# Layer 1's sums by node, as products of 32 columns in four quarters of the TensorE array

## The chip, the cores and the metric

The kernel runs on one core of one Trainium2 chip. The metric is the device time of one launch in microseconds; several runs are taken and their median is the kernel's time. All arrays are float32 unless said otherwise.

## The reference, cut to what matters

The reference is a stack of eight layers over 3125 nodes and 50,000 edges: four graph layers with a feed-forward (mixture) layer behind each. The edges arrive sorted by their receiving node. Two of the graph layers meet in the part of the kernel that is changed:

```python
def _L0_gnn_ref(h, weight, norm, src, dst, rel_type):
    transformed = jnp.einsum('ni,rio->rno', h, weight)      # 16 relations
    msg = transformed[rel_type, src] * norm
    return jax.ops.segment_sum(msg, dst, num_segments=h.shape[0])
...
def _L1_gnn_ref(node_z, node_feats, senders, receivers, edge_weight, edge_feats, ...):
    cut = 0.5 * (jnp.cos(edge_weight * jnp.pi / CUTOFF) + 1.0)
    cut = cut * (edge_weight < CUTOFF).astype(jnp.float32)
    W = (edge_feats @ W_dist + b_dist) * cut[:, None]
    x_j = embed_table[node_z][senders]
    msgs = x_j * W
    agg = jax.ops.segment_sum(msgs, receivers, num_segments=node_feats.shape[0])
    return jnp.concatenate([node_feats, agg], axis=1) @ W_comb + b_comb
```

`agg`, the sum of layer 1's messages by receiving node, is what the change is about. It needs nothing of layer 0's result, so the kernel computes it in the same pass over the edges as layer 0's sums.

## The kernel before, in words

**Stage one** (`stage_one`, L788) makes layer 0's graph sum, layer 0's mixture, layer 1's graph layer and the tables for layer 2, all in one loop. Nodes are cut into 25 tiles of 126 (the last holds 101), and a tile into 21 windows of six nodes (the last tile has 17), 521 windows in all. A window is the up to 128 edges that end in its six nodes; they lie one to a partition. A word table `tab` in DRAM holds for each node its normalised features and its embedding, 512 words.

For each window `k` the loop takes these steps:

- `fetch_rows` (L825): POOL starts an indirect DMA (the helper's line, L136) that gathers the 128 senders' rows of `tab` into a tile `g`. `G_BUFS` (L89) of these tiles go round, so the gathers run that many windows ahead, each as soon as the tile it takes is free.
- `fetch_feats` (L833): SP starts a DMA of the window's edge features into `f`, six windows ahead.
- `build` (L842): VectorE (DVE) builds two selection matrices, two windows ahead: `s0` (128 edges by 96 columns, six nodes by sixteen relations, weighted by `norm`; L850) and `s1` (128 edges by the 126 nodes of the tile, weighted by the cutoff; L852).
- `window` (L858): TensorE (PE) multiplies the two halves of the gathered features by `s0` into `c` (L866). ScalarE (ACT) copies `c` into `aT`, for two windows at a time (L870). PE multiplies the edge features by `W_dist` into `pw` (L873), and DVE multiplies `pw` by the gathered embeddings, in place in the second half of `g` (L875).
- `add_up` (L879), two windows behind: PE multiplies `s1` by that half of `g` and adds it up in a PSUM bank `agg` over the tile's windows (L884). After the last one ACT copies `agg` out to `ag` (L890).

After a tile's windows come eight `weigh` steps (L892): 32 products of `aT` with the sixteen relations' weights `w_rel` (L897). Windows and `weigh` steps together are 29 slots for a tile. In each slot `between` (L1117) takes a few steps of `route`, `experts` and `combine`, which carry the pairs of tiles already summed through layer 0's mixture and layer 1's second half, and steps of `background`, which finds where later tiles' edges begin and prepares the later layers.

The order in which each engine gets its work in this stage is the order in which this loop writes it (`tc.manual_schedule`); nothing is moved by a scheduler. PSUM has two buffers for `c`, two for `pw`, one for `agg`, one for the weighed sum `f` and two (`w`) for all the rest. After stage one the other layers follow, each after the last has been drained; the change does not touch them.

The part of the loop that fixes the order around the change, for a window step `j` of tile `t`:

```python
                build()
                window(k)
                if j >= 2:
                    add_up(k - 2)
                k += 1
```

The functions that the change touches, whole:

Of the kernel before, what the change touches and what calls it, by code (L numbers as in the profile page):

```python
# [9 lines left out]
F32 = mybir.dt.float32  # L10
# [3 lines left out]
OP = mybir.AluOpType  # L14
# [5 lines left out]
P = 128  # L20
N = 3125
NT = 25
NP = NT * P
NV = N - (NT - 1) * P
D = 256
# [20 lines left out]
TN = 126  # L46
TV = N - (NT - 1) * TN
NX = NT * TN
GN = 6
GC = TN // GN  # L50
GW = GN * 16
GL = -(-TV // GN)
# [3 lines left out]
F_SRC, F_CODE, F_NORM, F_DST, F_CUT, F_W0, F_W1, F_EID = range(8)  # L56
# [29 lines left out]
Q_SRC, Q_DST, Q_TYP, Q_W, Q_W1, Q_EW, Q_EID = range(7)  # L86
RW = 8

G_BUFS, F_BUFS = 10, 6  # L89
PERIOD = 2 * (GC + 8)  # L90
META_AT = 10
BG_EVERY = 3
# [3 lines left out]
def tile_gnn_ffn(ctx: ExitStack, tc: tile.TileContext, a: dict, out: bass.AP):  # L96
    nc = tc.nc
# [14 lines left out]
    def ps(tag, shape):  # L112
        return banks["pool"].tile(shape, F32, name=tag, tag=tag, bufs=banks["bufs"][tag])
# [21 lines left out]
    def gather(dst, table, idx):  # L135
        return nc.gpsimd.indirect_dma_start(  # L136
            out=dst, out_offset=None, in_=table, in_offset=bass.IndirectOffsetOnAxis(ap=idx, axis=0))
# [14 lines left out]
    iota_f = per.tile([P, P], F32, name="iota_f")  # L152
# [248 lines left out]
    for i in range(5):  # L401
        xg = pp.tile([P, 5, D], F32, name=f"n_x{i}")
        t = 5 * i
        m = 5 if i < 4 else 4
# [22 lines left out]
    for t in range(0, NT, 4):  # L427
        n = min(4, NT - t)
# [36 lines left out]
    with tc.If(uns > 0):  # L465

        rec = dram.tile([E, RW], F32, name="rec")
        with tc.tile_pool(name="srt", bufs=1) as ep, tc.tile_pool(name="srt2", bufs=2) as eb, \
# [25 lines left out]
            for b in range(ET // BT):  # L494
                s = slice(b * BT, (b + 1) * BT)
                n = BT * EP
# [9 lines left out]
                for i in range(BT):  # L506
                    j = b * BT + i
# [15 lines left out]
                at = eb.tile([EP, BT, 64], F32, name="s_attr")  # L523
# [137 lines left out]
    cur = start_norm(0)  # L661
# [3 lines left out]
    for i in range(5):  # L665
# [12 lines left out]
        cur = nxt  # L678
# [109 lines left out]
    def stage_one(late, cp, eb):  # L788
# [4 lines left out]
        def bank():  # L793
            return ps("w", [P, 2, D])
# [8 lines left out]
        def meta(t):  # L803
            pt = bank()[:, 0, :R1]
            nc.tensor.transpose(pt, raw.pop(t), ident[:R1, :R1])
            mt = eb.tile([P, 5, GC], F32, name="m_mt")
            si = eb.tile([P, GC], I32, name="m_si")
            un = eb.tile([P, GC], F32, name="m_un")
            nc.vector.tensor_copy(mt, pt.rearrange("p (f j) -> p f j", f=5))
            nc.vector.tensor_copy(si, mt[:, F_SRC])  # L810
            c, d, u = mt[:, F_CODE], mt[:, F_DST], mt[:, F_CUT]
            nc.vector.tensor_scalar_add(d, d, -float(TN * t))
            stt(c, c, -16.0 * TN * t, j96, op0=OP.add, op1=OP.subtract)

            nc.vector.tensor_tensor(un, d, j6, op=OP.is_lt)
            nc.vector.tensor_mul(u, u, un)
            mts[t], sis[t] = mt, si


        wins = [(t, j) for t in range(NT) for j in range(GL if t == NT - 1 else GC)]  # L820
        rows, feats, sums = {}, {}, {}
        agg_of = {}
        nxt = {"g": 0, "f": 0, "s": 0}
# [1 line left out]
        def fetch_rows():  # L825
            k = nxt["g"]
            if k < len(wins):
                nxt["g"] += 1
                t, j = wins[k]
                rows[k] = eb.tile([P, 2 * D], F32, name="g", bufs=G_BUFS)  # L830
                gather(rows[k], tab, sis[t][:, j : j + 1])

        def fetch_feats():  # L833
            k = nxt["f"]
            if k < len(wins):
                nxt["f"] += 1
                t, j = wins[k]
                feats[k] = eb.tile([65, P], F32, name="f", bufs=F_BUFS)
                v = nc.values_load(mixI[j : j + 1, t : t + 1], engines={EN.SP}, min_val=0, max_val=E)
                nc.sync.dma_start(feats[k], a["attr_t"][:, bass.ds(v, P)])  # L840

        def build():  # L842
            k = nxt["s"]
            if k < len(wins):
                nxt["s"] += 1
                t, j = wins[k]
                m = mts[t]
                s0 = eb.tile([P, GW], F32, name="s0", bufs=4)
                s1 = eb.tile([P, TN], F32, name="s1", bufs=5)
                nc.vector.tensor_scalar(s0, iota_f[:, :GW], m[:, F_CODE, j : j + 1], m[:, F_NORM, j : j + 1],  # L850
                                        op0=OP.is_equal, op1=OP.mult)
                nc.vector.tensor_scalar(s1, iota_f[:, :TN], m[:, F_DST, j : j + 1], m[:, F_CUT, j : j + 1],  # L852
                                        op0=OP.is_equal, op1=OP.mult)
                sums[k] = s0, s1

        cur = {}

        def window(k):  # L858
            t, j = wins[k]
            last = k + 1 == len(wins) or wins[k + 1][0] != t  # L860
            if j % 2 == 0:
                cur["c"] = ps("c0", [P, 2, D])
            pc, g = cur["c"], rows[k]
            o = (j % 2) * GW
            for h in range(2):
                nc.tensor.matmul(pc[:, h, o : o + GW], g[:, h * P : (h + 1) * P], sums[k][0], start=True, stop=True)  # L866
            if j % 2 or last:
                n = o // GW + 1
                b = (j - n + 1) * GN
                nc.scalar.copy(aT[:, :, :, b : b + n * GN].rearrange("p k r n -> p k n r"),  # L870
                               pc[:, :, : n * GW].rearrange("p k (n r) -> p k n r", r=16))
            pw = ps("pw", [P, D])
            nc.tensor.matmul(pw, feats.pop(k), wd, start=True, stop=True)  # L873
            fetch_feats()
            nc.vector.tensor_tensor(g[:, D:], pw, g[:, D:], op=OP.mult)  # L875

        ag_of = {}

        def add_up(k):  # L879
            t, j = wins[k]  # L880
            last = k + 1 == len(wins) or wins[k + 1][0] != t
            if j == 0:
                cur["agg"] = ps("agg", [P, D])
            nc.tensor.matmul(cur["agg"][:TN], sums.pop(k)[1], rows.pop(k)[:, D:], start=(j == 0), stop=last)  # L884
            fetch_rows()
            if last:
                q, i = t // 2, t % 2
                if i == 0:
                    ag_of[q] = eb.tile([P, 2, D], F32, name="ag", bufs=3)
                nc.scalar.copy(ag_of[q][:TN, i, :], cur["agg"][:TN])  # L890

        def weigh(t, i):  # L892
            if i == 0:
# [15 lines left out]
        def load_x(q):  # L909
            n = size(q)  # L910
            x = x_of[q] = eb.tile([P, 2, D], F32, name="x", bufs=3)
            if n == 1:
                nc.gpsimd.memset(x[:, 0, :], 0.0)
                nc.sync.dma_start(x[:TV, 0, :], a["x"][2 * q * TN :, :])
            else:
                nc.sync.dma_start(x[:TN], a["x"][2 * q * TN : 2 * (q + 1) * TN, :].rearrange("(t p) d -> p t d", p=TN))

        def load_e(q, i):
            n = size(q)
            e = e_of[q, i] = eb.tile([P, 2, D], F32, name=f"e{i}", bufs=1)  # L920
            nc.sync.dma_start(e[:TN, :n], rows126(ex, 2 * q, n)[:, :, i * D : (i + 1) * D])
# [214 lines left out]
        k = 0  # L1136
        for t in range(NT):
            n = GL if t == NT - 1 else GC
            for j in range(n):
                build()  # L1140
                window(k)
                if j >= 2:
                    add_up(k - 2)
                k += 1
                if j == 3 and t + 1 < NT:
                    raw[t + 1] = meta_load(t + 1, wb)
                if j == META_AT and t + 1 < NT:
                    meta(t + 1)
                if j == 14 and t % 2 == 0:
                    load_x(t // 2)  # L1150
                if j == 18 and t == 1:
                    beyond(eb, bank())
                if t % 2 and j == 19:
                    load_e(t // 2, 0)
                between()
            for i in range(8):
                weigh(t, i)
                if i < 2:
                    add_up(k - 2 + i)
                if i == 7 and (t % 2 or t == NT - 1):  # L1160
                    if t == NT - 1:
                        load_e(t // 2, 0)
                    flows.append(Flow(t // 2))
                between()
# [262 lines left out]
    with tc.tile_pool(name="f1", bufs=1) as fp, tc.tile_pool(name="f1b", bufs=2) as fb, psums(mm=3, y=3, tp=2):  # L1427
# [30 lines left out]
        for sh in range(28, -1, -4):  # L1458
            n = 8 if sh == 28 else 16
# [82 lines left out]
        for t in range(NT):  # L1542
            nc.tensor.matmul(pl.rearrange("p i k -> p (i k)"), fl[:, t, :], vals[:, t].rearrange("p i k -> p (i k)"),
                             start=(t == 0), stop=(t == NT - 1))
# [554 lines left out]
    with tc.tile_pool(name="g2", bufs=2) as gp, \  # L2099
# [60 lines left out]
        xin, rows = {t: At() for t in order2}, {t: [] for t in order2}  # L2160
# [118 lines left out]
        with tc.manual_schedule(engines={EN.PE, EN.DVE, EN.Activation, EN.Pool, EN.SP}):  # L2279
# [4 lines left out]
            last = pl.add(4, experts2())  # L2284
# [13 lines left out]
    with tc.tile_pool(name="w3", bufs=1) as wp:  # L2298
# [9 lines left out]
        with tc.tile_pool(name="g3", bufs=2) as gp, psums(tp=3, mm=4):  # L2308
# [24 lines left out]
            rows = {}  # L2333
            with tc.manual_schedule(engines={EN.PE, EN.DVE, EN.Activation, EN.Pool, EN.SP}):
                for r in range(ROWS):
                    look(r)
                for t in range(NT):
# [149 lines left out]
```

## Time and profile before

| | us |
|---|---|
| median of 3 runs | 3864.81 |
| lowest and highest run | 3861.73, 3865.3 |
| the profiled execution's own time | 3860.75 |
| its span, from the first to the last instruction | 3859.0 |
| first product of stage one (`c`), and the end of the last tile's `weigh` steps | 97.7, 1761 |
| PE busy in the span | 2721.7 (71%) |
| PE busy on `agg` in the span | 334.1 |
| DVE, ACT, POOL busy in the span | 1987.3 (51%), 846.0 (22%), 1724.6 (45%) |

Each row of the profile's list of groups names line, engine, operation, the tiles written and read, the shape and the count; then the busy time in us and the mean duration of one in ns; then how long the engine stood idle just before them, and what ended most of that. A product of float32 tiles shows as two instructions (passes), each with its own weight load ("PEld"). Since products are pipelined, the duration of one is not its price: the distance between the starts of two that follow each other is. TensorE's granted clock is given as a share of full speed.

### The profile page before, as it was taken

How to read it: one execution, taken by the hardware profiler on the slowest of the kernel's cores; microseconds unless marked ns; L12 is line 12 of the kernel's file. 1: busy time of each engine (PE TensorE's matmuls, PEld its weight loads, DVE VectorE, ACT ScalarE, POOL GpSimd, SP SyncE). 2: the span in 40 equal slices, each digit the busy share in tenths (PEclk: the TensorE clock that was granted, in tenths of full speed). 3: DMA queues.
4: the chain of work that ended last, by engine and by line, in shares of the span. 5: the costliest groups of instructions: out<-in, count | busy, mean ns of one | idle time of the engine just before them, and what ended most of it. 6: DMA issues, size and time to landing. Idle time of an engine off the chain costs nothing. (4 is left out here: it accounts for less than half of the span.)

```text
span 3859.0 us, 46777 instructions
## 1 busy us (share of the span) xinstructions
PE 2721.7 (71%) x13015; PEld 2250.7 (58%) x13015; DVE 1987.3 (51%) x7555; ACT 846.0 (22%) x1771; POOL 1724.6 (45%) x1971
## 2 busy tenths in 40 slices
PE   3788999999899999999384227748483112237994
PEld 2666788887788888887373115537361111225673
DVE  4446665776566555544423755656664333337411
ACT  2111232322122322323121002213231000014331
POOL 0342233352144333330024777777435777762343
PEclk9778999998899999999687557869695555557997
DMA  5756544553243444431122437768452333333563
GB/s 181 235 157 208 165 136 128 153 159 84 67 120 94 137 115 122 116 109 47 49 87 73 110 104 241 212 185 261 161 172 76 105 105 105 105 93 116 172 212 97
DMA packets 274479, 518.31 MB, mean 134 GB/s; under 512 B 53068, under 2 KB 176106, under 8 KB 274194
## 3 DMA queue, kind: packets, MB, share of 16 engines
q0 software_dynamic: 103744, 303.34, 26.9%
q1 hardware_dynamic: 159598, 201.27, 16.9%
q10 hardware_dynamic: 10852, 10.45, 0.8%
q8 instruction: 113, 1.85, 0.2%
q14 instruction: 172, 1.41, 0.1%
HBM read 428.07 MB, written 86.78 MB: 133 GB/s over the span
## 5 line engine op out<-in xcount | busy, mean ns | idle before, releaser
L136 POOL DMA_INDIRECT g<-tab,m_si x521 | 499.1, 958 | 1013.7 <-PE agg L884 262.4
L136 POOL DMA_INDIRECT g_rows<-tab,srcI x413 | 401.7, 973 | 130.6 <-issue 101.8
L136 POOL DMA_INDIRECT g_row<-tab,srcI x413 | 391.0, 947 | 132.2 <-issue 118.1
L866 PEld LDWEIGHTS c<-s,g 128*128 128x128 f32 x2084 | 332.5, 207 | 95.6 <-issue 38.7
L897 PE MATMUL f<-w_rel,aT 128*126 128x256 f32 x1600 | 377.2, 385 | 0.0
L866 PE MATMUL c<-s,g 128*128 128x96 f32 x2084 | 334.2, 286 | 51.2 <-DMA g<-tab,m_si 21.6
L870 ACT COPY aT<-c 128x384 f32<-128x384 f32 (+1 forms) x273 | 230.0, 842 | 607.0 <-PE c L866 573.4
L873 PE MATMUL pw<-w_d,f 65*128 65x256 f32 x1042 | 354.1, 424 | 0.0
L2342 DVE TENSOR_TENSOR ACC<-ACC,g_row 128x256 f32<-128x256 f32 x413 | 175.7, 425 | 341.5 <-DMA g_row<-tab,srcI 340.9
L884 PE MATMUL agg<-g,s 128*126 128x256 f32 x1042 | 334.1, 403 | 5.4 <-DVE g L875 5.4
L897 PEld LDWEIGHTS f<-w_rel,aT 128*126 128x126 f32 x1600 | 302.3, 191 | 48.3 <-issue 4.0
L1617 PE MATMUL tp<-ident,ACC 128*128 128x128 f32 x50 | 16.6, 435 | 422.3 <-DVE ACC L2342 422.3
L1947 PE MATMUL mm<-ro_xt,ro_w 128*128 128x192 f32 (+3 forms) x1152 | 265.0, 378 | 46.8 <-ACT ro_h L2012 25.0
L875 DVE TENSOR_TENSOR g<-pw,g 128x256 f32<-128x256 f32 x521 | 218.9, 420 | 120.0 <-PE pw L873 117.5
L1951 PE MATMUL y<-ro_w,ro_h 128*96 128x256 f32 (+2 forms) x1152 | 267.3, 384 | 0.0
L1617 PEld LDWEIGHTS tp<-ident,ACC 128*128 128x128 f32 x50 | 7.2, 204 | 429.8 <-issue 354.1
L1947 PEld LDWEIGHTS mm<-ro_xt,ro_w 128*128 128x128 f32 x1152 | 200.6, 205 | 95.0 <-ACT ro_h L2012 33.0
L884 PEld LDWEIGHTS agg<-g,s 128*126 128x126 f32 x1042 | 211.4, 203 | 40.2 <-DVE g L875 5.8
L1951 PEld LDWEIGHTS y<-ro_w,ro_h 128*96 128x96 f32 (+2 forms) x1152 | 200.2, 179 | 43.5 <-issue 1.0
L1015 PE MATMUL w<-w,b_h 128*126 128x256 f32 x800 | 211.7, 389 | 3.5 <-ACT xt L928 1.7
L1006 PE MATMUL w<-xt,w 128*128 128x252 f32 (+1 forms) x832 | 206.8, 372 | 3.0 <-ACT b_h L1008 1.3
L2222 DVE SCALAR_TENSOR_TENSOR ACC<-g_rows,g_e,ACC 128x256 f32<-128x256 f32 x413 | 201.5, 488 | 13.6
(582 smaller groups left out, 4674.2 us busy)
## 6 DMA issues: line engine op xcount, KB each, us to landing
ro_w<-in_L_ffn_blocks SPq DMA_DIRECT2D x72, 514.0 KB
ro_w<-in_L_ffn_blocks SPq DMA_DIRECT2D x72, 512.0 KB
f<-in_attr_t SPq DMA_DIRECT2D x521, 32.5 KB
xg<-zero SPq DMA_DIRECT2D x78, 200.0 KB
b_at<-in_edge_attr SPq DMA_DIRECT2D x100, 125.0 KB
tabr<-v SPq DMA_DIRECT2D x12, 758.0 KB
g<-tab,m_si POOLq DMA_INDIRECT x521
g_rows<-tab,srcI POOLq DMA_INDIRECT x413
```

What stands on the lines that cost most here:

```text
L136: return nc.gpsimd.indirect_dma_start(out=dst, out_offset=None, in_=table, in_offset=bass.IndirectOffsetOnAxis(ap=idx, axis=0))
L866: nc.tensor.matmul(pc[:, h, o : o + GW], g[:, h * P : (h + 1) * P], sums[k][0], start=True, stop=True)
L870: nc.scalar.copy(aT[:, :, :, b : b + n * GN].rearrange("p k r n -> p k n r"), pc[:, :, : n * GW].rearrange("p k (n r) -> p k n r", r=16))
L873: nc.tensor.matmul(pw, feats.pop(k), wd, start=True, stop=True)
L875: nc.vector.tensor_tensor(g[:, D:], pw, g[:, D:], op=OP.mult)
L884: nc.tensor.matmul(cur["agg"][:TN], sums.pop(k)[1], rows.pop(k)[:, D:], start=(j == 0), stop=last)
L897: nc.tensor.matmul(cur["f"][:TN], aT[:, h, r, :], wrel[:, h, r, :], start=(r == 0 and h == 0), stop=(r == 15 and h == 1))
L1006: nc.tensor.matmul(ph, w["01"][:, e, k, i * P : (i + 1) * P], xt[:, k, : n * TN], start=(k == 0), stop=(k == 1))
L1015: nc.tensor.matmul(py, last[:, k, i * TN : (i + 1) * TN], w["02"][:, e - 1, k, :], start=(k == 0), stop=(k == 1))
L1947: nc.tensor.matmul(ph, w[:, o : o + P], xt[:, k, :], start=(k == 0), stop=(k == 1))
L1951: nc.tensor.matmul(py, h[:, i, s], w[:, i * D : (i + 1) * D], start=(i == 0), stop=(i == self.fc - 1))
L2222: stt(u, g[:, r, :D], e[:, r0 + r : r0 + r + 1], u, op0=OP.mult, op1=OP.add)
```

## The change

The sums by node are made in three batches for a tile, and with narrower selection matrices.

- A window's six nodes lie, for all but two of the windows, within one block of 32 of the tile's nodes. `quarter(j)` names it: `6 j // 32`, and none for windows 5 and 10, which straddle two blocks. For the others `s1` has only the 32 columns of that block, and its product goes to those 32 partitions of `agg`. Windows 5 and 10 keep a selection matrix over all columns, now 128.
- The windows of a tile are taken in another order: 1, 2, 6, 7, 11, 12, 16, 17, then 3, 4, 8, 9, 13, 14, 18, 19, then 0, 15, 20, 5, 10. Within a batch the sums are issued so that neighbours lie in different quarters (1, 6, 11, 16, and so on).
- `add_up` runs once for a batch instead of once for a window: eight products behind the tenth window, eight behind the eighteenth, five behind the second `weigh` step.
- DVE writes the multiplied embeddings into a new tile `mt` (11 buffers) instead of into `g`, so a `g` tile is free after that multiplication, and the next gather is issued in `window`. `G_BUFS` goes from 10 to 9. The 32-column `s1` has 13 buffers, the wide one 3.
- `c` is still copied out two windows at a time where two neighbours follow each other; the last five windows of a tile are copied one at a time. ACT gets 48 instructions more by that (two for each of the 24 full tiles).

```diff
-G_BUFS, F_BUFS = 10, 6
+G_BUFS, F_BUFS = 9, 6
...
-        wins = [(t, j) for t in range(NT) for j in range(GL if t == NT - 1 else GC)]
+        batches = ((1, 2, 6, 7, 11, 12, 16, 17), (3, 4, 8, 9, 13, 14, 18, 19), (0, 15, 20, 5, 10))
+        together = (((1, 6, 11, 16), (2, 7, 12, 17)), ((3, 8, 13, 18), (4, 9, 14, 19)), ((0, 15, 20), (5,), (10,)))
+
+        def quarter(j):
+            return None if j in (5, 10) else GN * j // 32
+
+        wins, second = [], []
+        for t in range(NT):
+            for b in batches:
+                for j in b:
+                    if t < NT - 1 or j < GL:
+                        second.append(bool(wins) and wins[-1] == (t, j - 1) and not second[-1])
+                        wins.append((t, j))
...
-                s1 = eb.tile([P, TN], F32, name="s1", bufs=5)
+                a = quarter(j)
+                a, m1 = (0, P) if a is None else (32 * a, 32)
+                s1 = eb.tile([P, m1], F32, name=f"s1_{m1}", bufs=13 if m1 == 32 else 3)
...
-            nc.vector.tensor_tensor(g[:, D:], pw, g[:, D:], op=OP.mult)
+            mt = mults[t, j] = eb.tile([P, D], F32, name="mt", bufs=11), sums.pop(k)[1]
+            nc.vector.tensor_tensor(mt[0], pw, rows.pop(k)[:, D:], op=OP.mult)
+            fetch_rows()
...
-            nc.tensor.matmul(cur["agg"][:TN], sums.pop(k)[1], rows.pop(k)[:, D:], start=(j == 0), stop=last)
-            fetch_rows()
+            agg, begun = cur["agg"], b > 0
+            for js in together[b]:
+                js = [j for j in js if (t, j) in mults]
+                for j in js:
+                    a = quarter(j)
+                    mt, s1 = mults.pop((t, j))
+                    o = agg if a is None else agg[32 * a : 32 * a + 32]
+                    nc.tensor.matmul(o, s1, mt, start=not begun, stop=(j == 10), skip_group_check=True)
+                begun = True
...
                 window(k)
+                k += 1
                 if j >= 2:
-                    add_up(k - 2)
-                k += 1
+                    at = wins[k - 2][1]
+                    if at in (3, 0):
+                        add_up(t, 0 if at == 3 else 1)
...
-                if i < 2:
-                    add_up(k - 2 + i)
+                if i == 1:
+                    add_up(t, 2)
```

More of the change, by code (lines that the diff above doesn't have):

```diff
@@ L848, in build @@
                 s0 = eb.tile([P, GW], F32, name="s0", bufs=4)
-                s1 = eb.tile([P, TN], F32, name="s1", bufs=5)
+                a = quarter(j)
+                a, m1 = (0, P) if a is None else (32 * a, 32)
+                s1 = eb.tile([P, m1], F32, name=f"s1_{m1}", bufs=13 if m1 == 32 else 3)
                 nc.vector.tensor_scalar(s0, iota_f[:, :GW], m[:, F_CODE, j : j + 1], m[:, F_NORM, j : j + 1],
                                         op0=OP.is_equal, op1=OP.mult)
-                nc.vector.tensor_scalar(s1, iota_f[:, :TN], m[:, F_DST, j : j + 1], m[:, F_CUT, j : j + 1],
+                nc.vector.tensor_scalar(s1, iota_f[:, a : a + m1], m[:, F_DST, j : j + 1], m[:, F_CUT, j : j + 1],
                                         op0=OP.is_equal, op1=OP.mult)
@@ L859, in window @@
             t, j = wins[k]
-            last = k + 1 == len(wins) or wins[k + 1][0] != t
-            if j % 2 == 0:
+            if not second[k]:
                 cur["c"] = ps("c0", [P, 2, D])
             pc, g = cur["c"], rows[k]
-            o = (j % 2) * GW
+            o = GW if second[k] else 0
             for h in range(2):
                 nc.tensor.matmul(pc[:, h, o : o + GW], g[:, h * P : (h + 1) * P], sums[k][0], start=True, stop=True)
-            if j % 2 or last:
-                n = o // GW + 1
+            if second[k] or k + 1 == len(wins) or not second[k + 1]:
+                n = 2 if second[k] else 1
                 b = (j - n + 1) * GN
@@ L874, in window, with add_up @@
             fetch_feats()
-            nc.vector.tensor_tensor(g[:, D:], pw, g[:, D:], op=OP.mult)
[L877 to L882, printed above, removed]
-                cur["agg"] = ps("agg", [P, D])
-            nc.tensor.matmul(cur["agg"][:TN], sums.pop(k)[1], rows.pop(k)[:, D:], start=(j == 0), stop=last)
-            fetch_rows()
-            if last:
+            mt = mults[t, j] = eb.tile([P, D], F32, name="mt", bufs=11), sums.pop(k)[1]
+            nc.vector.tensor_tensor(mt[0], pw, rows.pop(k)[:, D:], op=OP.mult)
+            fetch_rows()
+        ag_of, mults = {}, {}
+        def add_up(t, b):
+            if b == 0:
+                cur["agg"] = ps("agg", [P, D])
+            agg, begun = cur["agg"], b > 0
[7 more added lines that the diff above has]
+                begun = True
+            if b == 2:
                 q, i = t // 2, t % 2
@@ L889, in add_up @@
                     ag_of[q] = eb.tile([P, 2, D], F32, name="ag", bufs=3)
-                nc.scalar.copy(ag_of[q][:TN, i, :], cur["agg"][:TN])
+                nc.scalar.copy(ag_of[q][:TN, i, :], agg[:TN])
         def weigh(t, i):
```

## The prediction

> **What bounds the kernel now.** I read the page's busy line and slices first, then stage one stretch by stretch, then the waits, then single products in the timeline. The slices place the stage: TensorE (PE) is at its fullest in slices 5 to 19 of 40 (one of them at 8), 96 us each.
>
> ```profile
> PE 2721.7 (71%) x13015; PEld 2250.7 (58%) x13015; DVE 1987.3 (51%) x7555; ACT 846.0 (22%) x1771; POOL 1724.6 (45%) x1971
> PE   3788999999899999999384227748483112237994
> PEclk9778999998899999999687557869695555557997
> ```
>
> The busy times by stretch of stage one (columns: stretch, length, busy us and instructions of PE, PEld, DVE, ACT, POOL, granted clock, DMA share, GB/s):
>
> ```profile
> 97.00:300.00 203.00, 156.25 (x606) 130.41 (x607) 96.27 (x386) 26.20 (x34) 80.77 (x86) 0.74 0.66 198
> 300.00:463.00 163.00, 145.25 (x670) 121.91 (x670) 104.24 (x343) 35.14 (x54) 49.92 (x52) 0.87 0.64 195
> 463.00:914.00 451.00, 444.98 (x2364) 389.60 (x2363) 299.45 (x1168) 121.20 (x214) 174.31 (x182) 1.00 0.48 138
> 914.00:1112.00 198.00, 180.96 (x852) 149.89 (x851) 114.98 (x506) 34.46 (x60) 48.97 (x51) 0.88 0.27 74
> 1112.00:1304.00 192.00, 183.86 (x977) 161.06 (x976) 123.37 (x534) 52.03 (x93) 81.43 (x109) 0.98 0.43 118
> 1304.00:1761.00 457.00, 456.49 (x2464) 403.00 (x2463) 249.45 (x981) 132.17 (x231) 154.69 (x162) 1.00 0.41 115
> ```
>
> PE is busy for 444.98 of 451 us in the third stretch and 456.49 of 457 in the last, at full clock; no other engine passes 67%. Busy PE rows are modelled, so I ask the waits too: from 1304 to 1761 none of PE's matrix products waits for anyone, from 463 to 914 all its waits come to 5.9 us. The two stretches are bound by PE. From 97 to 300 PE waits for chains of the planning (28.0 us on `startF`) and for one gather (21.6 us); there PE work is worth less. POOL's 262.4 us of waits for `agg` are for a free `g`, not a delay of PE.
>
> The price of a product is read from starts in the timeline (start us, us, engine, line, operation):
>
> ```profile
> 1405.40 0.60 PE L884 MATMUL agg<-g,s 128*126 128x256 f32 x2
> 1405.84 0.38 PE L982 MATMUL w<-ident,b_comb 126*8 126x126 f32 x2
> 1406.05 1.89 PE L897 MATMUL f<-w_rel,aT 128*126 128x256 f32 x8
> 1407.78 0.59 PE L884 MATMUL agg<-g,s 128*126 128x256 f32 x2
> ```
>
> Eight passes of 256 columns last 1.89 us; the last one 0.38 (mean 383 ns), so (1.89 - 0.38) / 7 = 0.216 us each. The two passes of `agg` (L884) take 1405.84 - 1405.40 = 0.44, about 0.43 us per window. Weight loads hide behind them.
>
> **What the Trainium skill says.** "TensorE: Matmul & The Clock Gate", "Part 3: Packing small matmuls — row/col tiling": products whose outputs lie in different groups of 32 partitions run at the same time, three such groups measured 2.38 times as fast; products still start and end strictly in program order. Nothing in this trace shows two groups at once. "TensorEngine Tiling (Array Packing)", "Key Properties": a change of the tiling mode drains TensorE. The trace speaks against a visible drain: the 8-column product L982 needs only the first 32 columns of the array, yet it starts 0.44 us after the two full passes ahead of it, and the full product behind it follows 0.21 us later, the streaming time of its own two passes of 126 columns. "PSUM — Partial Sum Buffer", "PSUM bank collisions raise a hardware error": different column tiles may write one bank at once, so `agg` in one bank is no obstacle; no run here shows it yet.
>
> **The change part by part.** I cost it per tile, on PE.
>
> *Removed*: 21 windows x 2 passes x 0.215 = 9.0 us per full tile.
>
> *Added*: the same 42 passes, 38 into one quarter and 4 over the whole array. Program order decides what can overlap. A window's two passes follow each other in the same quarter, so the second waits for the first; the next window's first pass, in another quarter, may start beside that second pass, but its second pass has again to wait. Not four but two run at once: n windows cost n + 1 passes instead of 2n. Each handover I price at 30 ns, the gap between one weight load and the next behind a finished pass, an estimate. Batches one and two: 8 x (0.215 + 0.03) + 0.215 = 2.18 us each; batch three: 3 x 0.245 + 0.215 + 4 x 0.215 = 1.81. Sum 6.2 us, so **2.9 us per tile** are saved (3.4 with free handovers, 1.9 with 80 ns, about the 84 ns that the smallest weight load lasts).
>
> *How much of it reaches the end.* Passes of L884 in each stretch, by 42, give the tiles: 2.5, 2.3, 7.1, 2.0, 3.0 and 7.7. Shares that I take: 0.5 in the first (waits of planning), 0.7, 0.75, 0.6, 0.75, and 0.95 in the last. The 0.75 is for DVE: a step's windows lose 0.43 us of PE each but keep their DVE work. In the windows of tile 10 (788.1 to 833.4) DVE is busy for 40.1 of 45.3 us; PE's 42.6 there would fall to about 38. In tile 23 (1666.7 to 1708.5) DVE has 27.5 of 41.8, enough room. Gains: 3.6 + 4.7 + 15.5 + 3.5 + 6.5 + 21.2 = **55 us**.
>
> *Small parts.* `s1` with 32 columns: L852 takes 343 ns for 126 columns, L1349, of the same kind, 293 for 25; some 50 x 521 = 26 us less for DVE, off the path except where DVE is late, and counted in the shares. The new tile `mt` costs DVE the same 421 ns. ACT: 48 more instructions, per full tile 8 x 876 + 5 x 517 instead of 10 x 876 + 517 ns, 0.3 us, hidden, ACT being 22% busy. One place is exposed: the first `weigh` product needs the last `aT` copy. Its chain is 0.28 (end of `c`) + 0.52 (copy) + two handovers of 0.05 = 0.9 us; before, `pw` and `agg` (0.11 + 0.43 + 0.43) covered it, now only `pw` does, 0.54 us, unless the slot has mixture work: at most 0.36 x 25 = 9 us, I take 0.1 x 25 and set it against DVE's relief. Gathers: `g` was held for two windows after use and 10 were there; now it is free after DVE's product and 9 are there, so in step k the gather of k + 9 is issued instead of k + 8: no shorter lead, same bytes, POOL's 0.96 us each unchanged. SP's loads of `f` stay at six ahead. The edge order changes no size.
>
> The profiled execution would go from 3860.75 to 3806; it lies 4 us under the median of the runs, 3864.8, from which I forecast **3810 us**.
>
> **The rivals.**
>
> 1. *All four quarters at once.* Were the two passes of a product no hindrance, a group of four costs two passes: 4 + 4 + 6 = 14 instead of 42 passes, 6.0 us per tile. DVE would then hold it back more; with shares 0.5, 0.5, 0.6, 0.5, 0.6, 0.9: 7.5 + 6.9 + 25.6 + 6.0 + 10.8 + 41.6 = 98 us, 3766. For it: the skill's group measurements. Against: program order and two passes.
> 2. *No overlap.* If float32 passes into different quarters run one by one, PE has its 42 passes as before, in lumps of 16 with DVE idle beside them, and the `aT` wait: 0 to 20 us more, 3865 to 3885, I take 3872. For it: no trace here shows an overlap.
> 3. *Slower: the weight loads come into the open.* In quarters each pass might have to wait for its own load, with no overlap. L982's loads of 8 columns last 84 to 88 ns, full ones 188; 32 columns by that line about 105. 38 x 0.105 = 4.0 us per tile, over 24.8 tiles and 85% bound, 85 us: 3950. The point from which it decides: a quarter's window costing more than the 0.43 us it costs now. Against it: L982's second load is hidden behind its first pass.
>
> **How the numbers follow.** Two at once: 0.55, from 3.4 us in all 24.6 tiles (84 us, 3781) to 1.9 us in 55% of them (26 us, 3839). Four: 0.12. No overlap: 0.18. Slower: 0.15. About 0.2%, 8 us, is what a measurement of this kernel tells from no change. Faster: 0.55 + 0.12 + 0.01 of the third = 0.68; same: 0.10 of the third; slower: 0.07 of it and 0.15 = 0.22. The range 3760 to 3890 takes in all of the first and third cases and some two thirds of the second; it leaves out the slow rival and the best end, 0.15 + 0.04.
>
> **What the profile after would show.** Right: the starts of `agg` passes alternate between near zero and about 0.22 us; eight windows take about 2.2 us from first to last; PE's busy time on `agg` falls by some 80 us; the windows of a late tile fall from 41.8 to about 38 us and its `weigh` steps grow by under 1 us; PE begins to wait for `s0`, `mt` or `pw` in tiles 6 to 14. Wrong: starts 0.22 apart throughout (no overlap), 0.3 or more (loads in the open), or four together. That DVE takes over would show in waits of PE for L866 and L891 of tens of us.

## The result: 1.8% faster

The changed kernel takes 3793.69 us (median of 4 runs, 3784.01 to 3801.29), the kernel before 3863.27 us beside it (4 runs, 3856.71 to 3865.3): a ratio of 0.9823, 95% interval 0.9804 to 0.9843. That is 70 us less, where 55 was forecast. The profiled execution of the changed kernel is its slowest, 3801.29 us with a span of 3799.6 us; the traces compared below are 59.4 us apart.

The page of the changed kernel, its busy line and the slices of PE and of the granted clock:

```profile
PE 2631.0 (69%) x13015; PEld 2107.1 (55%) x13015; DVE 1962.8 (52%) x7555; ACT 851.9 (22%) x1821; POOL 1723.9 (45%) x1971
PE   3778999999899999997482238577662112238994
PEclk9767999989899999999695559778785555557997
```

PE issues the same 13015 products and is busy for 90.7 us less. The nines of PE end a slice earlier. The last `weigh` product of stage one (by its line: duration in ns as least, median and most, then first and last start):

```profile
L920 PE MATMUL f<-w_rel,aT x1600: 377/379/791, 150.8 to 1712.9; 128*126 128x256 f32 x178
```

With the 0.215 us that a pass streams, stage one ends at 1713.1. In the kernel before the same row's last start is 1779.4, so its stage one ends at 1779.6. (The table ahead of the prediction gives 1761 for this; that is the end of the last tile's windows, ahead of its `weigh` steps.) Stage one is 66.5 us shorter, and what follows it 7 us longer (2086.5 against 2079.4), so the whole gain lies in stage one.

**How a batch runs on PE.** The timeline of the changed kernel at the end of a batch of eight windows in tile 21 (start, us, engine, line, operation; the bracket tells the idle time before and its releaser):

```profile
1507.70 0.62 PE L888 MATMUL pw<-w_d,f 65*128 65x256 f32 x2
...
1508.25 0.59 PEld L907 LDWEIGHTS agg<-mt,s 128*32 128x32 f32 x16 [0.33 <-issue]
1508.26 1.07 PE L907 MATMUL agg<-mt,s 128*32 128x256 f32 x16
...
1509.26 0.69 PE L881 MATMUL c<-s,g 128*128 128x96 f32 x4
```

The sixteen passes of the batch take 1509.26 - 1508.26 = 1.00 us to the start of the next product. Singly they would take 16 x 0.215 = 3.44. The same timeline, cut to the first 0.1 us of the batch, shows why:

```profile
1508.26 0.42 PE L907 MATMUL agg<-mt,s 128*32 128x256 f32 x4
```

Four passes have begun in that cut, all within 0.02 us. The single records start 6 to 7 ns apart in fours, and the fours 0.195 to 0.220 us apart: four waves of four. All four quarters work at once.

The other thing to see is the bracket: the weight loads wait 0.33 us for "issue". From the second pass of `pw` to the first of `agg` it is 0.310 us instead of 0.215; from the last of `agg` to the next full product 0.309 again; and that product's own second pass comes 0.19 us later where it is 0.11 elsewhere. So going into the quarters and out again (a trip, below) costs about 0.095 + 0.095 + 0.08, some 0.27 us for a batch.

**What a tile gains.** Here are three stretches of the kernel before: the windows of tile 20, those of tile 21, and tile 21's `weigh` steps (columns as ahead of the prediction). An even tile's windows carry more of the mixture's DVE work than an odd one's.

```profile
1484.90:1526.90 42.00, 41.83 (x240) 36.80 (x239) 32.36 (x137) 15.38 (x27) 18.18 (x19) 1.00 0.52 145
1545.80:1587.70 41.90, 41.90 (x239) 37.77 (x239) 27.53 (x104) 13.54 (x21) 18.70 (x20) 1.00 0.47 127
1587.70:1605.80 18.10, 18.10 (x86) 15.81 (x85) 2.04 (x6) 2.76 (x6) 2.38 (x3) 1.00 0.23 69
```

The same three of the changed kernel:

```profile
1435.60:1474.00 38.40, 36.70 (x234) 30.15 (x233) 30.95 (x137) 15.45 (x29) 19.65 (x21) 1.00 0.59 166
1493.80:1529.80 36.00, 36.00 (x232) 31.28 (x231) 26.14 (x99) 13.64 (x23) 19.97 (x21) 1.00 0.56 158
1529.80:1548.70 18.90, 18.90 (x92) 15.91 (x91) 2.75 (x11) 2.77 (x6) 1.06 (x2) 1.00 0.16 48
```

The odd tile falls from 60.0 to 54.9 us and PE never stops in it. The even tile's windows fall by only 3.6, and PE, busy for 41.83 of 42.00 before, now idles for 1.7 us of 38.40. What it waits for stands in the timeline of tile 20 of the changed kernel:

```profile
1442.70 0.70 PE L888 MATMUL pw<-w_d,f 65*128 65x256 f32 x2
...
1443.03 0.47 DVE L1040 SCALAR_TENSOR_TENSOR x<-w,b_comb,x 126x256 f32<-126x256 f32 x1
...
1443.80 0.16 DVE L210 SCALAR_TENSOR_TENSOR a_r<-a_q,a_r 126x2 f32<-126x2 f32 x1
1443.88 0.33 DVE L866 TENSOR_SCALAR s<-iota_f,m_mt 128x96 f32<-128x96 f32 x1
...
1444.26 0.69 PE L881 MATMUL c<-s,g 128*128 128x96 f32 x4 [0.86 <-DVE s L866]
```

DVE has mixture work (L1040, and a row of short steps up to L210) ahead of the selection matrix `s0` (L866), and `c` cannot start without it. In the kernel before, the longest distance between two starts on PE in that tile's windows was 0.41 us: a step had an `agg` product of its own, 0.43 us of PE work that needs nothing new of DVE. Here the distance ahead of 1444.26 is 1.24 us. Of the 1.7 us of waits in this tile's windows, two for `s0` make 1.24 (0.86 and 0.38); the third, 0.46, is one of the mixture for ACT's `xt`.

### The profile page after: what moved, and what is told of

It is laid out like the page before. It is cut to its first block, busy times and chain, and to the rows that moved or that the text cites. A ratio compares the mean times of both kernels' runs of the same rounds, so it can differ in the third digit from the quotient of the medians.

```text
span 3799.6 us, 46833 instructions
## 1 busy us (share of the span) xinstructions
PE 2631.0 (69%) x13015; PEld 2107.1 (55%) x13015; DVE 1962.8 (52%) x7555; ACT 851.9 (22%) x1821; POOL 1723.9 (45%) x1971
## 5 line engine op out<-in xcount | busy, mean ns | idle before, releaser
L881 PE MATMUL c<-s,g 128*128 128x96 f32 x2084 | 347.8, 294 | 67.6 <-DMA g<-tab,m_si 21.6
L888 PE MATMUL pw<-w_d,f 65*128 65x256 f32 x1042 | 365.9, 436 | 2.0 <-DMA f<-in_attr_t 2.0
L885 ACT COPY aT<-c 128x384 f32<-128x384 f32 (+1 forms) x323 | 237.7, 736 | 567.5 <-PE c L881 522.5
L891 DVE TENSOR_TENSOR mt<-pw,g 128x256 f32<-128x256 f32 x521 | 218.5, 419 | 95.2 <-PE pw L888 94.1
L1038 PE MATMUL w<-w,b_h 128*126 128x256 f32 x800 | 215.7, 394 | 6.7 <-ACT xt L951 4.5
L1040 DVE SCALAR_TENSOR_TENSOR x<-w,b_comb,x 126x256 f32<-126x256 f32 x200 | 96.0, 480 | 172.9 <-PE w L1038 172.2
L140 POOL DMA_INDIRECT xg<-XX,ro_pos x100 | 101.0, 1010 | 176.0 <-issue 74.4
```

Source lines behind the costliest of these rows:

```text
L891: nc.vector.tensor_tensor(mt[0], pw, rows.pop(k)[:, D:], op=OP.mult)
L1038: nc.tensor.matmul(py, last[:, k, i * TN : (i + 1) * TN], w["02"][:, e - 1, k, :], start=(k == 0), stop=(k == 1))
```

## The experiments

The theories are named as each expectation names them. Differences are against the changed kernel unless another is named. "End of stage one" is the last start of a `weigh` product plus 0.215 us, from each run's own trace.

### What the quarters are worth, and what the batches cost: e1_wide

```diff
-            return None if j in (5, 10) else GN * j // 32
+            return None
...
-G_BUFS, F_BUFS = 9, 6
+G_BUFS, F_BUFS = 8, 6
...
-                s1 = eb.tile([P, m1], F32, name=f"s1_{m1}", bufs=13 if m1 == 32 else 3)
+                s1 = eb.tile([P, m1], F32, name=f"s1_{m1}", bufs=12)
```

> The changed kernel with quarter() answering none for every window: same order of edges, same batches, mt tiles, but every selection matrix has 128 columns and every product of agg takes the whole array. To make room s1 has 12 buffers and G_BUFS is 8. Theory A (the gain is the overlap of the quarters on PE): 42 full passes per tile return, the time goes back to that of the kernel before or up to 20 us over it, 3863 to 3885, ratio 1.000 to 1.005. Theory B (the gain comes from g tiles that are free earlier and from batching, the quarters hardly matter): it stays within 15 us of the changed kernel, 3780 to 3810, ratio 0.978 to 0.986.

Measured: 3897.47 us (3894.37 to 3907.27) against 3858.39 for the kernel before, a ratio of 1.0100 (1.0083 to 1.0117). Stage one ends at 1814.6. The three stretches of above in this kernel:

```profile
1511.80:1555.00 43.20, 41.41 (x235) 35.57 (x233) 31.53 (x137) 15.45 (x29) 19.92 (x21) 1.00 0.52 147
1575.30:1615.80 40.50, 40.50 (x232) 36.69 (x231) 26.59 (x99) 13.68 (x23) 20.10 (x21) 1.00 0.50 140
1615.80:1635.20 19.40, 19.40 (x91) 16.96 (x90) 2.82 (x11) 2.76 (x6) 1.08 (x2) 1.00 0.15 47
```

This parts the change in two. The order of the edges, the batches and the buffers alone cost 39 us: theory B is out, and the cost lies above the 0 to 20 us that theory A gave. (`G_BUFS` is 8 here instead of 9. That doesn't show: PE waits for a gathered `g` once, 21.6 us, as in the kernel before and in the changed one.) In the odd tile they cost nothing: 1.3 us only move from the windows to `weigh`, and the sum stays at 59.9. In the even tile they cost 2.6: `weigh` gets 1.4 longer, but the windows, which should lose as much, get 1.2 longer, for PE now idles 1.8 us in them, with the same three pauses as the changed kernel (0.85 and 0.41 us for `s0`, 0.46 for `xt`). So the pauses come with the batches, not with the quarters. The quarters then take 60 - 54.9 = 5.0 us off the odd tile and 63.5 - 58.2 = 5.3 off the even one, in all 104 us (3897.5 to 3793.7). (The narrow `s1` also takes DVE less, 317 ns instead of 349; in the odd tile, where PE never stops, that doesn't enter.)

### Does the order within a batch matter: e2_neighbours

Neighbours in the order now share a quarter (1 and 2, 6 and 7, and so on), so that products taken strictly in turn could not run four at once.

```diff
-        together = (((1, 6, 11, 16), (2, 7, 12, 17)), ((3, 8, 13, 18), (4, 9, 14, 19)), ((0, 15, 20), (5,), (10,)))
+        together = (((1,), (2,), (6,), (7,), (11,), (12,), (16,), (17,)), ((3,), (4,), (8,), (9,), (13,), (14,), (18,), (19,)), ((0, 15, 20), (5,), (10,)))
...
-                    nc.tensor.matmul(o, s1, mt, start=not begun, stop=(j == 10), skip_group_check=True)
-                begun = True
+                    nc.tensor.matmul(o, s1, mt, start=(b == 0 and j in (1, 6, 11, 16)), stop=(j == 10), skip_group_check=True)
```

> The changed kernel with the products of a batch in the order 1, 2, 6, 7, 11, 12, 16, 17, so that two neighbours share a quarter; the sums are the same. Theory A (only neighbours in different quarters run at once; a product waits for the one before it in its own quarter and nothing overtakes it): eight windows take 9 to 12 passes of 0.215 us instead of 4, so 1.1 to 1.7 us more in each of 50 batches, some 80% of it at the end: 45 to 70 us, 3840 to 3865, ratio 0.994 to 1.000. Theory B (PE finds by itself what can run at once): within 10 us of the changed kernel.

Measured: 3793.7 us (3787.14 to 3797.08), ratio 0.9826 (0.9810 to 0.9843): the time of the changed kernel. A cut of its timeline through the first 0.1 us of a batch:

```profile
1503.09 0.44 PE L907 MATMUL agg<-mt,s 128*32 128x256 f32 x4
```

Still four at once; their starts are 11 to 15 ns apart instead of 6 to 7, as theory B has it. So the order in which the kernel writes the products of a batch does not limit what overlaps. Whether the compiler or PE's own queue brings the fours together, these runs do not tell; the records do not name the window of a pass.

### How much DVE takes back: e3_after_const and e4_before_const

In both, `s1` is not built; a tile of ones takes its place in the sums (in the second, against the kernel before). DVE loses its work on `s1`, everything else in stage one stays. The sums are then others, later layers route by them and do more work, so only stage one's trace can be compared.

```diff
-                s1 = eb.tile([P, m1], F32, name=f"s1_{m1}", bufs=13 if m1 == 32 else 3)
-                nc.vector.tensor_scalar(s1, iota_f[:, a : a + m1], m[:, F_DST, j : j + 1], m[:, F_CUT, j : j + 1],
-                                        op0=OP.is_equal, op1=OP.mult)
-                sums[k] = s0, s1
+                sums[k] = s0, ones[:, :m1]
```

> The changed kernel without the building of s1 for each window (a constant tile of ones stands in for it, so the sums of layer 1 are left out as such): DVE loses 521 instructions of 0.29 us, 151 us, PE keeps all its products. Theory A (DVE has become late in the windows of many tiles and takes back part of PE's gain): 15 to 45 us faster than the changed kernel, 3750 to 3780. Theory C (only PE's own changes of array mode stand between the gain and its ideal): 0 to 5 us.

> The control for the same: the kernel before without the building of s1 (ones stand in for it, so the sums of layer 1 are left out as such). DVE loses 521 instructions of 0.345 us, 180 us. Theory A (before, PE was the bound and DVE had room): 0 to 15 us faster than before, ratio 0.996 to 1.000, clearly less than the same cut gives the changed kernel. Theory C: the same gain in both kernels.

Measured: the whole times, 5844.05 and 7001.71 us, say nothing. Stage one ends at 1688.9 instead of 1713.1, and in the kernel before at 1767.3 instead of 1779.6: 24 us less after the change, 12 before it, within theory A's ranges of both. These are traces of single executions; against e2_neighbours, which takes the changed kernel's time and ends stage one at 1709.0, the 24 are 20. Tile 20's windows in the first of the two:

```profile
1414.60:1451.90 37.30, 36.14 (x235) 30.04 (x233) 26.76 (x116) 15.46 (x29) 19.76 (x21) 1.00 0.59 171
```

37.3 instead of 38.4; the odd tile's stay at 36.0. DVE's work on `s1` thus costs stage one 20 to 24 us after the change, about twice what it costs before. It isn't all of the even tile's loss: the same pause, from 1421.60 here, is still 1.01 us.

### More batches, no full products, earlier building: e5_split, e7_quarters, e8_ahead, e9_both

These ran on another chip, on which the kernel before takes 4299.94 us; the changed kernel was not run on it, so they are compared with one another and with the kernel before, and what was expected against the changed kernel can't be decided here.

e5_split makes the first two batches in two calls of four products each, one window apart:

```diff
-                    if at in (3, 0):
-                        add_up(t, 0 if at == 3 else 1)
+                    if at in (3, 4, 0, 15):
+                        add_up(t, 0 if at in (3, 4) else 1, 0 if at in (3, 0) else 1)
```

> The changed kernel with each of the first two batches of a tile added up in two calls of four products, one window apart, so two more changes of the array's mode in and out for each tile and the same products. Theory A (a change into quarters and back costs PE what the changed kernel's trace shows: 0.09 us at the entry, 0.09 and 0.08 at the exit): 2 x 0.26 x 25 tiles = 13 us, some 80 to 100% of it at the end: 10 to 13 us slower than the changed kernel, 3800 to 3810. Theory D (the lumps of eight products are what makes DVE late and PE wait): smaller lumps give the 13 us back, 3785 to 3797.

e7_quarters gives windows 5 and 10 a 64-column `s1` and two quarter products each instead of a full one (`5.5` stands for the second half of window 5):

```diff
-            return None if j in (5, 10) else GN * j // 32
+            return GN * j // 32
...
-((0, 15, 20), (5,), (10,)))
+((0, 5.5, 15, 20), (5, 10, 10.5)))
...
-                a, m1 = (0, P) if a is None else (32 * a, 32)
+                a, m1 = 32 * a, 64 if j in (5, 10) else 32
```

> The changed kernel with windows 5 and 10 as two quarter products each (s1 of 64 columns, its halves into two neighbouring quarters), so the third batch has seven quarter products and no full one. Theory A (four quarters run at once, and each change of mode costs): the third batch goes from two waves, a change of mode of 0.2 us and four full passes (0.43 + 0.2 + 0.86) to four waves (0.86): 0.63 us less per tile, 25 tiles, some 85%: 11 to 15 us faster than the changed kernel, 3778 to 3783. Theory D (DVE's lateness sets the end, PE's savings no longer count): within 4 us of the changed kernel.

e8_ahead builds the selection matrices three windows ahead; e9_both is e7_quarters with four ahead:

```diff
-        for _ in range(2):
+        for _ in range(3):
             build()
...
-                s0 = eb.tile([P, GW], F32, name="s0", bufs=4)
+                s0 = eb.tile([P, GW], F32, name="s0", bufs=5)
```

> The changed kernel with the selection matrices built three windows ahead instead of two (s0 with 5 buffers, the narrow s1 with 14). DVE has the same work. Theory A (PE waits for s0 because DVE gets to it late in the windows, by order): 5 to 15 us faster, 3779 to 3789. Theory D (it is DVE's amount of work in those tiles, not its order): within 4 us.

> Windows 5 and 10 as two quarter products each, and the selection matrices built four windows ahead (s0 with 6 buffers, the narrow s1 with 15). Theory A: both gains add up, 16 to 30 us faster than the changed kernel, 3764 to 3778. Theory D: less than 8 us.

| kernel | us | ratio to before (interval) | end of stage one |
|---|---|---|---|
| e5_split | 4280.74 | 0.9965 (0.9953 to 0.9977) | 1805.4 |
| e7_quarters | 4265.32 | 0.9924 (0.9900 to 0.9948) | 1775.4 |
| e8_ahead | 4277.28 | 0.9951 (0.9937 to 0.9965) | 1783.1 |
| e9_both | 4271.12 | 0.9946 (0.9929 to 0.9963) | 1770.9 |

Building further ahead on top of e7_quarters brings nothing (4271.12 against 4265.32, intervals overlapping). It does bring `s0` in time: in stage one `c` waits for it 20.2 us, 18 times, in e7_quarters, and never in e8_ahead or e9_both. But the wait comes back one product later. `pw` has two buffers, and PE now waits for DVE to read one of them (`mt`): 67.8 us, 51 times, in e9_both and 57.0 in e8_ahead, instead of 10.6. In tile 20, PE in e7_quarters, then in e9_both:

```profile
1502.11 0.69 PE L881 MATMUL c<-s,g 128*128 128x96 f32 x4 [0.85 <-DVE s L866]
1502.65 0.48 PE L888 MATMUL pw<-w_d,f 65*128 65x256 f32 x1
```

```profile
1496.71 0.58 PE L881 MATMUL c<-s,g 128*128 128x96 f32 x4
1498.27 0.48 PE L888 MATMUL pw<-w_d,f 65*128 65x256 f32 x1 [0.97 <-DVE mt L891]
```

Tile 20 begins at 1493.49 in the first and at 1489.11 in the second, and this `pw` starts 9.16 us into the tile in both. So the late `s0` is not the cause by itself: in these steps DVE is behind with all of its work, which is nearer to theory D of e8_ahead (the amount of work) than to theory A (its order).

### The same beside the changed kernel, and one engine for another: e10_after, e11_split, e13_quarters, e12_act

A third chip; the kernel before takes 4277.99 us on it. e10_after is the changed kernel, e11_split and e13_quarters are e5_split and e7_quarters again. e12_act is e13_quarters with `s1` made by ScalarE (ACT) in two steps:

```diff
-                nc.vector.tensor_scalar(s1, iota_f[:, a : a + m1], m[:, F_DST, j : j + 1], m[:, F_CUT, j : j + 1],
-                                        op0=OP.is_equal, op1=OP.mult)
+                sq = eb.tile([P, m1], F32, name=f"sq_{m1}")
+                nc.scalar.activation(sq, iota_f[:, a : a + m1], AF.Square, bias=neg[t][0][:, j : j + 1])
+                nc.scalar.activation(s1, sq, AF.Relu, bias=m[:, F_CUT, j : j + 1], scale=neg[t][1][:, j : j + 1])
```

> The changed kernel itself once more, beside the next three on one chip, so that they can be compared with it: ratio 0.980 to 0.986 to the kernel before if the chip is as that of its first runs; on a chip like that of e5, e7, e8 and e9, where the kernel before takes 4300, theory A expects its gain to be smaller (PE waits more there), 0.990 to 0.996.

> The kernel of e5 (each of the first two batches added up in two calls of four products) beside the changed kernel on one chip. Theory A (a change of the array's mode costs PE about 0.26 us in and out, 50 more of them): 10 to 13 us slower than the changed kernel of the same call. Theory D (smaller lumps give it back): within 4 us of it or faster.

> The kernel of e7 (windows 5 and 10 as two quarter products each) beside the changed kernel on one chip. Theory A: 0.63 us of PE per tile, 11 to 15 us faster than the changed kernel of the same call. Theory D (DVE's lateness sets the end): within 4 us of it.

> The kernel of e7 with s1 made on ScalarE instead of DVE, in two instructions (the square of the difference, then a ReLU of cutoff minus cutoff times it, which is the same 0-or-cutoff matrix), for two small DVE instructions more per tile. DVE loses 521 instructions of 0.29 us, 151 us, and the sums keep their values. Theory A (DVE is late in the windows of many tiles): 12 to 25 us faster than e7's kernel of the same call. Theory C (DVE is no bound, ACT's 1042 instructions more delay the copies of aT): 0 to 20 us slower than it.

| kernel | us | ratio to before (interval) | end of stage one |
|---|---|---|---|
| e10_after | 4252.31 | 0.9947 (0.9925 to 0.9969) | 1781.1 |
| e11_split | 4257.24 | 0.9952 (0.9938 to 0.9967) | 1805.8 |
| e13_quarters | 4243.98 | 0.9929 (0.9901 to 0.9956) | 1771.0 |
| e12_act | 4224.96 | 0.9896 (0.9862 to 0.9930) | 1789.0 |

- *Splitting a batch*: the medians are 5 us apart, within the intervals, between the 10 to 13 of theory A and the 4 of theory D. The traces' stage one is 24.7 us longer, but the profiled execution of e11_split is the slowest of its 15 (4270.91), that of e10_after is near its median (4250.59). In the odd tile 23 the windows grow from 37.3 to 37.9 us: 0.6 for two more trips into the quarters, 0.3 each, which is what the starts showed. The even tiles grow by 2 to 4 us, and there it is another wait: from 1370 on the mixture's `w` (L1038) waits for ACT's `b_h` three times, 5.2 us in all, against 1.1 us in e10_after.
- *No full products*: stage one 10 us shorter in the traces, with 0.5 to 0.6 us off each tile's `weigh` steps (18.9 to 18.4 and 19.8 to 19.2). The total is 8 us less, its interval overlapping, between theory A's 11 to 15 and theory D's 4.
- *`s1` on ScalarE* gives the lowest median of all, 19 us under e13_quarters, in theory A's range of 12 to 25, though the intervals overlap a little. Four of its six runs lie at 4223 to 4225 and two at 4259 to 4261; the profiled one is of the second kind, and its stage one isn't shorter. That the gain comes from DVE's relief is therefore not shown. The rows of the moved work, line 873 and 874 of that kernel, then `s0`:

```profile
L874 ACT ACTIVATE s<-sq,m_mt,m_nu 128x32 f32<-128x32 f32 x521 | 216.5, 416 | 18.5 <-PE agg L913 0.7 <-issue 0.3
L870 DVE TENSOR_SCALAR s<-iota_f,m_mt 128x96 f32<-128x96 f32 x521 | 174.6, 335 | 0.0
L873 ACT ACTIVATE sq<-iota_f,m_nd 128x32 f32<-128x32 f32 x521 | 162.5, 312 | 47.6 <-DVE m_nu L820 17.5 <-DMA ex<-zero 9.2 <-DMA f<-in_attr_t 5.9
```

ACT pays 379 us for what cost DVE 161; it can, being busy for 27% of that span.

*The changed kernel gains less on this chip*: 26 us, 0.5%, instead of 70, within the 0.990 to 0.996 expected for such a chip. Between the trace of e10_after and that of the first chip, stage one is 68 us longer and what follows it 381 (2467.8 against 2086.5), with nearly the same DVE busy time (1958.6 and 1962.8). What differs is "issue", time in which an engine waited for nothing that the profile shows. The waits of that kind that the view of waits lists add up in stage one to 46.7 us of DVE and 93.2 of ACT here, against none and 8.2 on the first chip; after it to 334.5 of PE and 206.7 of DVE, against 8.8 and 7.7. The other seven kernels on the two later chips show much the same (41 to 59 us of DVE in stage one). What stands behind it is not shown, and the kernel before has no trace there, so where the 44 us went is open. The figures in this document are for the first chip except where one of the last eight kernels is named.

## Why the prediction was right, and where it was not

The forecast of 3810 us with the range 3760 to 3890 holds the measured 3793.69, and the sign is right. The working is not, and that the total came so near was luck. The quarters took off 104 us (e1_wide to the changed kernel), where the pairs of the forecast could take off at most 71. The batches cost 39 us, where the shares, meant for DVE and for the waits of planning, took 16 off the 71. These errors, 33 and 23 us, stood against each other.

1. **"Program order decides what can overlap. ... Not four but two run at once"** failed. The trace shows fours, and e2_neighbours shows that the order written within a batch doesn't decide. The mechanism was that of the first rival, to which the text gave 0.12. Per tile it forecast 2.9 us (pairs) or 6.0 (fours); the quarters measured 5.0 and 5.3, between e1_wide and the changed kernel. The Trainium skill, which says in "Part 3: Packing small matmuls — row/col tiling" of "TensorE: Matmul & The Clock Gate" that products in different groups run at once and gives 2.38 for three, was right on the first; for four groups this trace has sixteen passes in 1.00 us instead of 3.44, which is 3.4 times, or 2.9 with the whole trip counted (3.44 in 1.17). The strict order that it states there was my reason for pairs; whether the starts keep it no run here shows. I took from a rule on starts and ends a rule on overlap, and left a window's second pass to block the next window's first.
2. **"The trace speaks against a visible drain"** failed. The Trainium skill, "TensorEngine Tiling (Array Packing)", "Key Properties", says that a change of mode drains TensorE, and the trace after agrees: 0.31 us instead of 0.215 on the way in and on the way out, about 0.27 us for a batch with the late second pass. Three batches make 0.8 us a tile, and 6.0 - 0.8 = 5.2 lies between the measured 5.0 and 5.3. The inference from L982 was bad: a transpose of eight columns shows no such gap, and so tells nothing of products that are sent to a quarter. In the tile's view:

```profile
L907 PEld LDWEIGHTS agg<-mt,s x1042: 106/110/333, 115.1 to 1699.1; 128*32 128x32 f32 x173, 128*128 128x128 f32 x1
L907 PE MATMUL agg<-mt,s x1042: 379/379/796, 115.1 to 1699.4; 128*32 128x256 f32 x173, 128*128 128x256 f32 x1
...
  issue: 40.8, 113
```

   The loads' price for 32 columns was well estimated (105 ns; 110 at the median) and stays hidden. The 40.8 us of "issue" ahead of them are not the price of the trips: in most of such a wait PE still streams the passes before (of the 0.33 us at 1508.25 the products lost 0.095). 75 batches at 0.27 us are 20 us.

3. **The batches' own cost** was mis-sized. It stood in the sum as shares (55 of a possible 71 us) and 0.1 us a tile for `aT`; e1_wide measured 39 us. The text named the right loser, DVE's `s0`, but priced it as DVE's busy share over a tile. In tile 20 that share is 81% (30.95 of 38.40), which looks like room enough. What counts is the stretch of a few steps in which DVE has more to do than PE: there PE waits for `s0` or, when `s0` is built earlier, for a buffer of `pw`. That the `agg` product of the step used to fill such a gap, and that its going is what costs, is argued from the two timelines (longest distance 0.41 and 1.24 us); no run puts it back alone, and smaller lumps (e11_split) brought nothing back. PE's waits from 463 to 914 in the changed kernel (us, times, longest):

```profile
PE c L881 <- DVE s L866: 3.9, 5, 1.6
PE c L881 <- issue: 3.9, 3, 2.0
PE w L1335 <- DVE k_cum L1331: 3.0, 1, 3.0
PE c L881 <- ACT aT L885: 2.6, 3, 1.0
PE pw L888 <- DMA f<-in_attr_t: 2.0, 1, 2.0
PE agg L907 <- DVE mt L891: 1.7, 1, 1.7
```

   All are a few us, as forecast for DVE not taking over; from 1304 to 1713 `c` waits 4.6 us for `s0`, where before it waited for nobody. Not all of the even tiles' loss stands in such rows.

4. **The sum by stretch.** Tiles 0 to 4 gained 8.1 us (forecast 3.6 + 4.7), tiles 5 to 11 8.9 (15.5), 12 and 13 10.6 (3.5), 14 to 16 8.9 (6.5), 17 to 24 30.1 (21.2). That is 66.5 against 55. The worst miss is in tiles 10 and 11, which lost 7.6. Some of it is a wait: ahead of one `agg` product PE stood 1.7 us for `mt`. Most of it belongs to this one execution: e2_neighbours, with the same time, lost 0.5 there. Its tile 11 takes 60.2 us, that of the changed kernel's trace 65.1, and from 840 to 860 the granted clock was 1.00 there and 0.74 here. Why the clock fell was not tested.

5. *Small parts.* The drop of a late tile's windows from 41.8 "to about 38" was 36.0, the growth of `weigh` "under 1 us" was 0.8, PE's busy time on `agg` fell by 229 us (334.1 to 105.2) instead of 80, since the busy time of four passes at once counts once. `mt` costs DVE what the product in place cost (419 and 420 ns), and `s1` 317 ns on average instead of 350, which makes 17 us less for DVE and not 26. ACT has 50 instructions more, not 48. None of the 85 us of exposed loads of the slower rival came, and the second rival's "no overlap" is refuted by the first fence of the timeline; its 0 to 20 us for lumps was at most half of the 39 that the batches cost.

## What to carry to other kernels

Products with few output columns are worth gathering into runs over all four quarters of the array: here eight float32 products of 32 columns took the time of 2.3 full ones, or 2.7 with the whole trip counted. Make the runs long, since each trip costs some 0.27 us, and keep full products out of them. Before moving a product out of a step, look at what it covered there: in e1_wide 1.3 us of products left the even tile's windows, and these grew by 1.2 us, with DVE busy for 73% of them. When PE waits for one operand of a late engine, bringing that operand forward can move the wait to the next one: look at how much that engine has to do in the stretch.

## What the hardware showed that I had not expected

- Two passes of one float32 product don't hinder products in other quarters: sixteen passes run as four waves of four, 0.195 to 0.220 us apart, also when neighbours in the program share a quarter.
- A trip into the quarters and out again costs about 0.27 us on PE, with no wait listed for the products themselves; in the timeline it stands as "issue" ahead of the weight loads (0.33 us).
- Three chips took 3858.39, 4277.99 and 4299.94 us for the same kernel before, and the gain of the same change was 1.8% on one and 0.5% on another. In stage one of the changed kernel the view of waits lists none of DVE for "issue" on the first and 46.7 us on the second.
